# Storing a layer's reciprocals row by row instead of once per pair

## The chip, the core and the metric

The kernel runs on one core of a Trainium2 chip. The metric is the device time of a run in microseconds. Before the change the median of three runs is 3098.26 us (3097.44 to 3100.63).

## The reference

Two attention layers with residuals on x of shape (1, 128, 256, 256), read as 128 rows of 256 tokens with 256 channels, each over a group norm of the whole input. The change is in layer 1:

```python
def _L1_conv_ref(x, w_in, b_in, w_out, b_out, band):
    ...                                     # NUM_HEADS = 4, D = 64, F = 256 tokens
    qkv = x2 @ w_in.T + b_in
    q, k, v = jnp.split(qkv, 3, axis=-1)
    ...
    scores = jnp.einsum('bhid,bhjd->bhij', q, k) / jnp.sqrt(jnp.asarray(D, x.dtype))
    keep = jnp.abs(i - j) <= band           # band = 16
    scores = jnp.where(keep, scores, -jnp.inf)
    attn = jax.nn.softmax(scores, axis=-1)
    out = jnp.einsum('bhij,bhjd->bhid', attn, v)
    ...
    y = out @ w_out.T + b_out

x = x + _L0_conv_ref(_gn(x), ...)
x = x + _L1_conv_ref(_gn(x), ..., 16)
```

The sum of the exponentials of each token and head divides its output. The kernel takes the reciprocal of that sum, and keeps it for a check at the end.

## The kernel before

The kernel has a fast version, `fast_kernel`, and a general one that runs only where checks on the numbers fail; only the fast one runs here. Layer 0 writes its result x1 to memory. Layer 1, from about 1980 us on, works on *pairs* of rows (`NP` = 64 pairs). Everything in its loop is ordered by hand: every engine gets its instructions in the order of the program, and SyncE issues all of the loop's transfers from one queue, in that order too.

A pair p goes through four turns of the loop:

- As `n3` (turn p-3) it is made: `Pair1.__init__` issues its loads, four of 128 KB into `xs` (line 1930, in runs of 32 floats), which has 3 buffers, and one of 512 KB into `xt` (line 1935), which has 6. In the same turn, some three quarters through it, `turn` transposes `xs` on VectorE (line 1943).
- As `nn` it is normalised (`centre`, line 1948) and its differences and biased residual are made on GpSimd.
- As `nxt` its q, k and v come from seven products each (`product`, lines 1995 and 1999; `join`, line 2015).
- As `now` it has its scores (line 2052, rows 0 and 1), the exponentials and the mask by the band, and `apply(0)` for row 0: outputs (line 2077) and sums (line 2085). `invert(0)` takes the reciprocal of row 0's sums into `rv[:, 0, :]` (line 2108) and `weigh(0)` multiplies (line 2113). These two are the last of the turn in the program.
- As `was`, in the turn after, it has `apply(1)`, `invert(1)` and `weigh(1)` for row 1, and its output projection (line 2170). As `old` the residual is added on GpSimd (line 2186) and the result stored (line 2187).

The order of SyncE's work in a turn p of the loop is therefore: the loads of pair p+3, the output of pair p-2 (waits for GpSimd), and in `weigh(1)` the store of both rows' reciprocals of pair p-1 into `rsum1` (line 2118). The store takes every 32nd partition of `rv`, 4 partitions of 2 KB. A few turns before the end `load_sums` reads all of `rsum1` back for the check. The last `LATE` = 8 pairs check their reciprocals in place and store nothing.

On TensorE a turn has two stretches of many small instructions: both `scores` with `was.apply(1)` at its start, and `now.apply(0)` in its middle. The rest are larger products.

Of the kernel before, what the change touches and what calls it, by code (L numbers as in the profile page):

```python
# [16 lines left out]
P = 128  # L17
# [4 lines left out]
def bcast(ap, axis, n):  # L22

    ap = ap.unsqueeze(axis)
    shape = list(ap.shape)
    shape[axis] = n
    return ap.broadcast_to(shape)
# [746 lines left out]
def fast_kernel(  # L774
# [25 lines left out]
    nc = tc.nc  # L800
# [9 lines left out]
    NP = S // 2  # L810
# [1031 lines left out]
    DH = P // H1  # L1842
    QB = 32
    LATE = 8
    rsum1 = dram.tile([NP, H1, 2, I], F32, name="rsum1")
    with tc.tile_pool(name="l1", bufs=2) as sb, tc.tile_pool(
# [74 lines left out]
        class Pair1:  # L1921
# [188 lines left out]
            def weigh(self, r):  # L2110
                rv, odd = self.rv, self.odd
                oT = sb.tile([P, 2, I], F32, name="oT1", tag="oT", bufs=3)
                nc.vector.tensor_tensor(oT, odd, bcast(rv[:, r, :], 1, 2), ALU.mult)
                self.oT[r] = oT
                if self.p >= NP - LATE:
                    look(late, self.rv[:, r, :], 1e-16)
                if r == 1 and self.p < NP - LATE:
                    nc.sync.dma_start(rsum1[self.p].rearrange("q r i -> q (r i)"), rv[0:P:DH].rearrange("q r i -> q (r i)"))

            def out_row(self, r):  # L2120
                for b in range(NB):
# [91 lines left out]
        def look(queue, src, lo):  # L2213

            at = cols[0]
            cols[0] += 1

            def low():
                above = sm.tile([P, I], F32, name="above", tag="above", bufs=1)[:, : src.shape[1]]
                nc.vector.tensor_scalar(above, src, lo, None, ALU.is_gt)  # L2220
                nc.vector.tensor_reduce(ok[:, 0, at : at + 1], above, AX.X, ALU.min)

            queue += [lambda: nc.vector.tensor_reduce(ok[:, 1, at : at + 1], src, AX.X, ALU.max), low]
# [238 lines left out]
```

## Time and profile before

| | |
|---|---|
| median of three runs | 3098.26 us |
| time of the profiled execution | 3098.43 us |
| its span on the chip | 3096.7 us |
| TensorE matmul busy | 2991.3 us (97%) |
| TensorE weight load busy | 2088.0 us (67%) |
| VectorE busy | 2374.1 us (77%) |
| ScalarE busy | 1656.8 us (54%) |
| GpSimd busy | 2587.0 us (84%) |
| granted TensorE clock, mean | 0.987 |
| moved by DMA | 328.06 MB in 690787 packets |

In the profile PE is TensorE's matmuls, PEld its weight loads, DVE is VectorE, ACT ScalarE, POOL GpSimd and SP SyncE; a q behind an engine's name stands for its sequencer, which issues transfers. L2118 is line 2118 of the kernel. A row of waits has the instruction that waited, what ended the wait, the sum in us, how often and the longest. A row of the timeline has the start, the duration, the engine, the line and the tiles, written from read. "+9.2" in the text stands for 9.2 us after the first matmul of a pair's scores; pairs are counted by the turn in which they are `now`.

### The profile page before, as it was taken

The page shows a single profiled execution, that of the slowest core. Times are in us where ns is not written, and L with a number is a line of the kernel's source. Part 1 is how long each engine was busy: PE and PEld are TensorE (multiplying, and loading weights), DVE is VectorE, ACT ScalarE, POOL GpSimd, SP SyncE. Part 2 cuts the span into 40 slices and gives each one's busy share as a digit, 9 for nine tenths or more (in the row PEclk, how much of TensorE's full clock was granted, in tenths as well). Part 3 has the DMA queues.
Part 4 walks back from the last instruction along what each step waited for, and adds up shares of the span by engine and source line. Part 5 has one row for each costly group of instructions (what it writes and reads, how often), then busy time and mean ns, then how long its engine had stood idle before and what let it go on. Part 6 is the DMA issues. An engine that isn't in the chain of part 4 may idle for free.

```text
span 3096.7 us, 83063 instructions
## 1 busy us (share of the span) xinstructions
PE 2991.3 (97%) x34386; PEld 2088.0 (67%) x34386; DVE 2374.1 (77%) x4075; ACT 1656.8 (54%) x2887; POOL 2587.0 (84%) x1950
## 2 busy tenths in 40 slices
PE   6689999999999999999999999899999999999998
PEld 4355555665555655555655555588888888888886
DVE  7987677777777777777777777688887877777787
ACT  3454544444444444444444444366666666666664
POOL 3469899898898888898888898588888888888885
PEclk9799999999999999999999999999999999999999
DMA  9952333323333332333333233433434343434341
GB/s 357 390 190 53 100 70 100 95 65 93 100 97 73 96 90 67 100 97 91 78 89 95 73 97 87 112 89 93 99 90 104 86 105 85 105 92 97 94 100 44
DMA packets 690787, 328.06 MB, mean 106 GB/s; under 512 B 538624, under 2 KB 639872, under 8 KB 689248
## 3 DMA queue, kind: packets, MB, share of 16 engines
q1 hardware_dynamic: 686000, 320.02, 38.8%
q8 instruction: 273, 4.47, 0.6%
q10 hardware_dynamic: 4400, 2.63, 0.3%
q14 instruction: 114, 0.93, 0.1%
HBM read 253.83 MB, written 68.74 MB: 104 GB/s over the span
## 4 chain that ended last, share of the span: by engine, by line
PE 89%; DVE 4%; DMA 4%; POOL 1%; issue 1%; ACT 1%; SPq 0%; ACTq 0%; POOLq 0%; DVEq 0%
PE ps_p L1364 21%; PE ps_qk L1999 12%; PE ps_sc L1401 9%; PE ps_ov L1436 8%; PE ps_v L1382 7%; PE ps_y L1490 7%; PE ps_su_y L2170 6%; PE ps_qk L1995 6%; PE ps_o L2077 4%; PE ps_su L1444 3%; PE ps_sc L2052 3%; PE ps_su_y L2085 2%; DMA xa<-in_x_dram 2%; DMA zt<-in_z_dram 1%; DVE st L1199 1%
## 5 line engine op out<-in xcount | busy, mean ns | idle before, releaser
L1425 POOL TENSOR_TENSOR eboth<-e 128x512 f32<-128x512 f32 x512 | 744.2, 1475 | 174.2 <-PE ps_su L1444 95.2
L1421 DVE TENSOR_TENSOR e<-ps_sc,eb 128x1024 f32<-128x1024 f32 x384 | 458.2, 1221 | 288.7 <-ACT ps_sc L1413 288.6
L1413 ACT ACTIVATE ps_sc<-ps_sc 128x1024 f32<-128x1024 f32 x384 | 375.4, 1007 | 435.8 <-PE ps_sc L1401 310.0
L2063 POOL TENSOR_TENSOR e<-e,bw 128x384 f32<-128x384 f32 x256 | 276.6, 1111 | 77.4 <-ACT e L2061 77.4
L1401 PE MATMUL ps_sc<-qT,kT 32*128 32x256 f32 x4096 | 293.9, 400 | 0.0
L1401 PEld LDWEIGHTS ps_sc<-qT,kT 32*128 32x128 f32 x4096 | 185.5, 184 | 101.5 <-issue 91.5
L1490 PEld LDWEIGHTS ps_y<-wo,oT 128*128 128x128 f32 x1024 | 194.2, 190 | 81.8 <-issue 44.0
L1436 PE MATMUL ps_ov<-e,v 128*32 128x256 f32 x4096 | 247.6, 382 | 1.1 <-DVE v L1388 1.1
L1364 PE MATMUL ps_p<-xnT,wq 128*128 128x512 f32 x512 | 247.5, 605 | 0.1
L1364 PE MATMUL ps_p<-xgT,wg 128*128 128x512 f32 x512 | 247.3, 605 | 0.0
L1490 PE MATMUL ps_y<-wo,oT 128*128 128x256 f32 x1024 | 242.0, 379 | 1.7 <-POOL oT L1480 1.7
L1382 PE MATMUL ps_v<-wv,xnT 128*128 128x256 f32 x1024 | 241.8, 379 | 0.0
L1364 PE MATMUL ps_p<-xnT,wk 128*128 128x512 f32 x512 | 240.7, 592 | 0.0
L1382 PEld LDWEIGHTS ps_v<-wv,xnT 128*128 128x128 f32 x1024 | 194.5, 190 | 54.0 <-issue 30.9
L2008 ACT ACTIVATE u<-ps_qk,bin_c 128x256 f32<-128x256 f32 x378 | 174.7, 477 | 93.0 <-PE ps_qk L1999 93.0
L2108 DVE RECIPROCAL rv<-sums 128x256 f32<-128x256 f32 x128 | 223.0, 1742 | 0.0
L1436 PEld LDWEIGHTS ps_ov<-e,v 128*32 128x32 f32 x4096 | 120.0, 109 | 109.4 <-issue 41.5
L1116 POOL TENSOR_TENSOR zrs<-zrs,mhalf 128x32 f32<-128x32 f32 (+1 forms) x19 | 87.9, 4631 | 114.4 <-DVE zrs L1109 114.4
L1371 ACT ACTIVATE gT<-ps_p,bg_c 128x512 f32<-128x512 f32 x128 | 87.9, 687 | 175.1 <-PE ps_p L1364 175.1
L1364 PEld LDWEIGHTS ps_p<-xnT,wk 128*128 128x128 f32 x512 | 97.2, 190 | 122.8 <-issue 122.6
L1999 PE MATMUL ps_qk<-dT,wst 128*128 128x256 f32 x756 | 173.5, 379 | 0.0
L1364 PEld LDWEIGHTS ps_p<-xnT,wq 128*128 128x128 f32 x512 | 91.9, 189 | 114.0 <-issue 112.0
(254 smaller groups left out, 7061.1 us busy)
## 6 DMA issues: line engine op xcount, KB each, us to landing
xa<-in_x_dram SPq DMA_DIRECT2D x8, 4096.0 KB
xt<-in_x_dram SPq DMA_DIRECT2D x64, 512.0 KB
x<-xo SPq DMA_DIRECT2D x16, 2048.0 KB
xt<-x SPq DMA_DIRECT2D x64, 512.0 KB
rvb<-rsum SPq DMA_DIRECT2D x252, 128.0 KB
xs<-x SPq DMA_DIRECT2D x252, 128.0 KB
out_dram<-yo SPq DMA_DIRECT2D x63, 512.0 KB
xs<-in_x_dram SPq DMA_DIRECT2D x248, 128.0 KB
```

The source lines that it names most:

```text
L1364: nc.tensor.matmul(ps, w[:, k, m * P : (m + 1) * P], getattr(self, src)[:, k, :], start=(k == 0), stop=(k == KC - 1),)
L1382: nc.tensor.matmul(self.ps_v[:, b * C : (b + 1) * C], self.xnT[:, k, t * P : (t + 1) * P], wv[:, k, :], start=(k == 0), stop=(k == KC - 1),)
L1401: nc.tensor.matmul(self.pss[q // 2][:, q % 2, b, :], self.kT[rs, c, r * I + b * P : r * I + (b + 1) * P], self.qT[rs, c, r * I : (r + 1) * I],
L1413: nc.scalar.activation(self.pss[a], ps, AF.Exp)
L1421: nc.vector.tensor_tensor(es[a], pss[a], eb[:, h : h + 2], ALU.mult)
L1425: nc.gpsimd.tensor_tensor(t, es[a][:, :, 0, :], es[a][:, :, 1, :], ALU.add)
L1436: nc.tensor.matmul(ov[q * D0 : (q + 1) * D0, c, :], self.v[:, r, b, h * D0 : (h + 1) * D0], es[q // 2][:, q % 2, b, :], start=(b == 0), st ...
L1490: nc.tensor.matmul(self.ps_y[:, b * C : (b + 1) * C], self.oT[r][:, k, b * P : (b + 1) * P], wo[:, k, :], start=(k == 0), stop=(k == KC - 1),)
L1995: nc.tensor.matmul(to[:, at], rhs[:, at], lhs, start=start and b == 0, stop=True, skip_group_check=True)
L1999: nc.tensor.matmul(to, lhs, rhs, start=start, stop=True, skip_group_check=True)
L2063: nc.gpsimd.tensor_tensor(e[:, q], e[:, q], bcast(bw.rearrange("p b w -> p (b w)"), 1, KC), ALU.mult)
L2108: nc.vector.reciprocal(self.rv[:, r, :], self.sums)
```

## The change

The store of a pair's reciprocals is no longer made once, with row 1. `weigh` stores its own row each time: row 0 at the end of turn p, and row 1 in the middle of turn p+1.

```diff
                 if self.p >= NP - LATE:
                     look(late, self.rv[:, r, :], 1e-16)
-                if r == 1 and self.p < NP - LATE:
-                    nc.sync.dma_start(rsum1[self.p].rearrange("q r i -> q (r i)"), rv[0:P:DH].rearrange("q r i -> q (r i)"))
+                if self.p < NP - LATE:
+                    nc.sync.dma_start(rsum1[self.p][:, r, :], rv[0:P:DH, r, :])
```

SyncE's order in a turn p becomes: the loads of pair p+3, the output of pair p-2, row 1 of pair p-1, row 0 of pair p. The bytes that are stored are the same.

## The prediction

> **What bounds the kernel now.** First the page: the busy shares and the chain of work that ended last.
>
> ```profile
> PE 2991.3 (97%) x34386; PEld 2088.0 (67%) x34386; DVE 2374.1 (77%) x4075; ACT 1656.8 (54%) x2887; POOL 2587.0 (84%) x1950
> ...
> q8 instruction: 273, 4.47, 0.6%
> ...
> PE 89%; DVE 4%; DMA 4%; POOL 1%; issue 1%; ACT 1%; SPq 0%; ACTq 0%; POOLq 0%; DVEq 0%
> ```
>
> TensorE is nearly always busy, and the chain is TensorE. A change to loads can only pay where TensorE stands still, so I ask where that is inside layer 1. The timeline gives the start of each pair's scores (L2052): 2400.96, 2418.39, 2435.13, 2451.88 us. Most pairs take exactly 16.74 us, the others 16.8 to 18.4. From pair 2 (2026.33) to pair 56 (2945.64) there are 54 pairs in 919.31 us, against 54 x 16.74 = 903.96: **15.35 us are lost**, 0.5% of the run. The waits of TensorE's weight loads from 2010 to 3010 us, and the chain around one slow pair (number 50, start 2842.69), say to what:
>
> ```profile
> PEld ps_o L2077 <- issue: 24.0, 70, 1.0
> ...
> PEld ps_su_y L2085 <- issue: 9.0, 13, 1.4
> ```
> ```profile
> 2851.10 0.31 PE ps_su_y L2085 x8
> 2851.41 1.06 issue
> 2852.47 0.52 PE ps_su_y L2085 x6
> ```
>
> "issue" means that the engine waited for nothing that the profile shows. It falls in the middle of `apply` (L2077, L2085), never on a row that names a load. I take it for instruction fetch: the DMA share by slices of time around that stop (columns: PE, PEld, DVE, ACT, POOL busy, clock, DMA share, GB/s) has one lone packet ahead of it,
>
> ```profile
> 2846.19:2849.94 3.75, 3.75 (x19) 3.13 (x17) 3.07 (x5) 2.39 (x6) 3.75 (x4) 1.00 0.00 0
> 2849.94:2850.94 1.00, 1.00 (x71) 0.84 (x75) 0.99 (x3) 1.00 (x3) 0.91 (x1) 1.00 0.06 16
> 2850.94:2851.44 0.50, 0.47 (x23) 0.10 (x8) 0.50 (x2) 0.45 (x1) 0.00 (x0) 1.00 0.00 0
> 2851.44:2852.44 1.00, 0.00 (x0) 0.00 (x0) 0.30 (x1) 0.00 (x0) 0.55 (x1) 1.00 0.63 216
> ```
>
> and that packet is of queue 8, "instruction", 16 KB. Listing the packets of queue 8 against TensorE's records: a pair has 622 records, a fetch comes every 256 or so, and 7 pairs (4354) are 17 fetches plus 2 records, so the pattern repeats every seventh pair. Each time TensorE stops it goes on 2.2 to 2.7 us after the start of the latest fetch (pair 50: fetch at 2850.08, on at 2852.47), and always 384 to 388 records after the same point of the stream. So a fetch needs about 2.35 us before its instructions can run. It hurts only where 256 instructions run faster than that: in the **first burst** (both scores and `apply(1)`, 0 to 3 us into a pair) and the **second** (`apply(0)`, about 8.0 to 9.4 us into it).
>
> Where the loads are today: SyncE's part of the timeline,
>
> ```profile
> 2409.14 0.38 SPq L2187 DMA_DIRECT2D out_dram<-yo  x1
> 2409.62 0.54 SPq L2118 DMA_DIRECT2D rsum<-rv  x1
> 2410.21 2.93 SPq L1930 DMA_DIRECT2D xs<-x  x4
> 2413.18 1.98 SPq L1935 DMA_DIRECT2D xt<-x  x1
> ```
>
> Pair 24 began at 2400.96, so the loads are issued 9.25 us into it, 55% through. By the packets, the out store moves from +9.1 to +10.8, xs from +10.8 to +14.3 or, with a fetch in between, +15.9, and xt until +15.9 to +17.4. From there to +9 of the next pair the DMA engines do nothing but fetch: **both bursts now have the engines to themselves**.
>
> **What the Trainium skill says.** "Runtime: NRT & Kernel Launch", Instruction fetch mechanics: instructions come in blocks of 16 KiB (256), which the engine's sequencer fetches by its own DMA queue while it runs the block before. The trace agrees: 4.47 MB in 273 packets is 16.4 KB each, and 68,772 matmuls and weight loads over 256 make 269. "DMA: Bandwidth & Descriptors", Anatomy of one DMA: a wait for a semaphore is held by the issuing sequencer, not by the DMA engines. The trace agrees: nothing on SyncE passes the out store while it waits for POOL (483.9 us in all). Same page, Queues, rings and completion order: a DMA engine takes turns between queues packet by packet, a packet being 9 to 17 descriptors as a rule and at most 64. No row here shows the packets' size; that fetches do start amid 128-byte descriptors, the trace shows (19 of them, below).
>
> **The change part by part.** *Stores.* One store of 8 KB for a pair becomes two of 4 KB: 56 more issues of about 0.54 us (L2118), 30 us of SyncE. SyncE waits up to 8.6 us in a pair for the out store's data, so they cost nothing; without that cover SyncE would still have 16.74 us for 0.38 + 2 x 0.54 + 2.93 to 4.2 + 0.66 to 2.0, under 8. The row-0 store reads a row that the second reciprocal doesn't write; were that wait there all the same, it would have from +3.7 to +5.8, where the reciprocal of row 1 starts (2441.00 in pair 26, begun 2435.13).
>
> *The new wait.* The row-0 store stands at the end of a pair's program and waits for `invert(0)`, whose reciprocal ends 3.17 us into the next pair by the clock (pair 26: 2436.56 + 1.74), or 2.18 from pair 27 on, where the checks ahead of it have run out. Queued behind it on SyncE: four xs loads and the xt load of the coming pair, then the out store and the row-1 store. So the xs loads move from +9.25 of one pair to +3.8 (+2.8) of the next, **11 to 12 us later**, not sooner.
>
> *Who waits for them.* The transpose (L1943) reads xs 12.8 us into the pair. Now: four issues, then data 0.9 us after the first (out store: 2409.14, data +9.1), 3.5 to 5.1 us of it: landed at +8.2 to +9.8. At least 3 us are left: cost 0. xt is read a pair later: 0. The out store waits for POOL until +8.2 and now also for the xt issue, until +7.4 to +9; its buffer is written again a pair later: 0.
>
> *What the loads now lie beside.* xs moves from about +4.7 to +8.2 (+3.7 to +7.2), xt and the out store until about +12: across the second burst. Fetches that start there and have nothing to spare: pairs 8, 15, 22, 29, 36, 43, 50 (at +6.83 to +7.40; TensorE on at +9.2 to +9.8), and pair 1 by the same count: **8 fetches**. Those of the next family (pairs 3, 10 ... 52, at +7.2 to +8.5) are wanted 0.9 to 2.1 us after they are usable: 0.
>
> Price of one delay: the trace has no tight fetch under load, so bounds. 4096 descriptors over 16 engines in 3.5 us are 13.7 ns each: 17 of them 0.23 us, 64 of them 0.88 us. For the lower end: the packet of a fetch itself took 0.88 to 1.1 us mostly in the 128-byte stream as on idle engines. A gain is excluded: the engines are idle there today. I take half the ceiling, 0.4 us: 8 x 0.4 = **+3.2 us** (1.8 to 7.0).
>
> What is given back: in the first burst three fetches (pairs 21, 26, 33) start within 0.05 us of the end of xt. At 0.1 us each: **-0.3 us**. Sum +2.9 us on the profiled execution's 3098.43 (span 3096.7); that one is 0.17 above the median 3098.26, so on the median: 3101.
>
> **The rivals.**
> *Slower, clearly:* a fetch is held until the 128-byte stream has passed, instead of taking turns. Then the 8 fetches wait from about +7.0 to +8.2 or later, 1.2 to 2 us each: +10 to +16, **3110**. It decides from 0.78 us a fetch (6.2 / 8). For it: fetches of pairs 13 and 55 come 0.6 to 1.2 us later than their place in the stream suggests, with loads in flight. Against: 19 fetches start at +9.9 to +12.9 amid load.
> *No effect:* fetches pass at no cost. **3098.3**. For it: their unchanged length under load.
> *Faster:* the tail of xt is what holds the first burst's fetches, which start anywhere from +16.5 to +0.85. If all nine late ones started at +16.5, they would give back 5.2 us, and shorter packets (six take 1.2 to 1.3 rather than 0.95 us) 1.9 more: **3091 to 3093**. Against: most start 0.2 to 1.1 us after the last load has ended, and those at +16.5 start just after `join` frees the bank for `scores(1)`, so it is TensorE's sequencer that is late.
> *Loads too late* for the transpose: a microsecond per pair, about **3150**; 3 us of margin speak against it. That the change doesn't move the loads: SyncE is in order, so only if the reciprocal were not last; it is.
>
> **How the numbers follow.** A measurement of this kernel tells about 0.2% (6.2 us) from no change. Small cost 0.45 (0.07 of it beyond 0.2%), no effect 0.15, held fetches 0.21, faster 0.16 (0.13 beyond 0.2%), late loads 0.03. Faster 0.13, same 0.38 + 0.15 + 0.03 = 0.56, slower 0.07 + 0.21 + 0.03 = 0.31. The range, 3093 to 3110, takes in both ends of the delay's price, most of the faster case and half of the held fetches.
>
> **What would show it.** SyncE's timeline: store, four xs and xt at +2.8 to +3.8, no wait of the transpose on a DMA; the pair's floor still 16.74; in every seventh pair a stop in L2085 that is longer by 0.2 to 0.9 us; the first burst's stops as before. I am wrong if the floor of all pairs moves, if pairs without a tight fetch begin to stop in the second burst, or if the first burst's stops go.

## The result, and the profile after

**3106.14 us** (median of ten runs, 3102.42 to 3112.05) against 3098.49 for the kernel before (3096.68 to 3100.78): a ratio of **1.0025**, 95% interval 1.0017 to 1.0033. The change makes the kernel 7.6 us slower, and its runs spread more than twice as wide. The profiled execution took 3109.16 us (span 3107.4), in the upper half of the ten, so its differences are larger than the median's.

The first lines of the page, and the waits of TensorE's weight loads from 2010 to 3010 us for which the profile shows no releaser:

```profile
PE 2984.2 (96%) x34386; PEld 2085.0 (67%) x34386; DVE 2374.1 (76%) x4075; ACT 1657.2 (53%) x2887; POOL 2585.3 (83%) x1950
...
q8 instruction: 273, 4.47, 0.6%
```
```profile
PEld ps_o L2077 <- issue: 26.5, 71, 1.0
...
PEld ps_su_y L2085 <- issue: 13.4, 12, 2.8
...
PEld ps_qk L1999 <- issue: 10.9, 27, 1.9
```

The work and the 273 instruction blocks are the same, and the granted clock, taken over the whole run, is no lower (0.989 for 0.987). Longer are the stops in L2085, the end of `apply` (13.4 us for 9.0), and in L1999, the products behind it (10.9 for 7.5 over the same stretch before). SyncE's timeline shows where the loads went; columns are start and duration in us, issuer, line, transfer and how often:

```profile
2391.45 0.38 SPq L2187 DMA_DIRECT2D out_dram<-yo  x1
2391.94 11.80 SPq L2118 DMA_DIRECT2D rsum<-rv  x2
2403.79 2.76 SPq L1930 DMA_DIRECT2D xs<-x  x4
2406.60 0.72 SPq L1935 DMA_DIRECT2D xt<-x  x1
2408.20 0.38 SPq L2187 DMA_DIRECT2D out_dram<-yo  x1
```

Pair 24 starts at 2400.02. The two stores (row 1 of a pair, then row 0 of the next, which waits 11 us) stand in one row, and the loads come 3.77 us into the pair instead of 9.25. From pair 27 on it is 2.80.

The floor of a pair is still 16.74 us, and no transpose waits for a DMA: the profile lists no wait before L1943. (VectorE waits for an output store to leave its buffer four times, 2.0 us in all, and never before the change; the prediction put this at nothing, and the chain of work does not pass through it.) The time is lost in the pairs with a stop. Their sums over the floor, from the starts of the scores:

| pairs | before | after |
|---|---|---|
| 8, 15, 22, 29, 36, 43, 50 | 8.25 us | 18.96 us |
| the other 47 from 2 to 55 | 7.05 us | 8.28 us |

So +10.7 of the profiled execution's +10.7 us lie in seven pairs; the rest (+1.2 in the other pairs, +1.1 in pairs 56 to 60, -2.5 ahead of pair 2) cancels. Of the -2.5, 1.2 is pair 1, which takes 16.74 us for 17.95: it has a fetch at +3.1 where it had one at +7.8, and no stop. The long pieces in which the chain of work after the change stood at "issue" (start, us) are one in every seventh pair, 15 to 50; before, only one piece of this chain, of 1.06 us in pair 50, was long enough to be listed:

```profile
2252.94 1.29 issue
2373.40 1.29 issue
2493.77 2.13 issue
2615.05 1.04 issue
2735.11 2.16 issue
2858.60 2.43 issue
```

Pair 43 (start 2726.12) by slices of time, and the chain through it:

```profile
2732.12:2733.37 1.25, 1.25 (x8) 1.09 (x7) 1.25 (x2) 0.54 (x2) 1.25 (x1) 1.00 1.34 208
2733.37:2733.87 0.50, 0.50 (x11) 0.17 (x16) 0.50 (x1) 0.39 (x1) 0.50 (x1) 1.00 0.43 63
2733.87:2734.87 1.00, 1.00 (x75) 0.88 (x76) 0.99 (x4) 1.00 (x3) 0.41 (x1) 1.00 1.09 383
2734.87:2735.37 0.50, 0.23 (x9) 0.00 (x0) 0.50 (x1) 0.21 (x1) 0.00 (x0) 1.00 0.69 238
```
```profile
2734.80 0.31 PE ps_su_y L2085 x9
2735.11 2.16 issue
2737.26 0.75 PE ps_su_y L2085 x5
2738.01 3.34 PE ps_qk L1999 x8
```

The last three numbers of a slice are the granted clock, the DMA share and GB/s. xs runs out at 2733.4, and just as the second burst begins xt takes every engine (share 1.09, 383 GB/s). The instruction fetch of this pair starts at +8.65 (2734.77) by the packets of queue 8, when xt is nearly through; in the kernel before it started at +6.82 on idle engines. TensorE goes on 2.5 us after that start, as ever. The eight products behind the stop take 3.34 us where they took 1.92 in the same pair before:

```profile
2734.13 1.92 PE ps_qk L1999 x8
```

There is no gap between these products; TensorE runs slowly. The granted clock, third from the end in the slice that follows, is at half for 3.41 us from just after the stop, which costs some 1.7 us:

```profile
2737.42:2740.83 3.41, 3.41 (x12) 2.35 (x8) 0.42 (x1) 1.63 (x4) 1.73 (x3) 0.50 0.03 8
```

In this profile it happens in layer 1's loop only here, and not after the stops of pairs 29 and 50, which are as long; the last section says what sets them apart.

### The profile page after: what moved, and what is told of

It reads as the page before. It is cut to its first block, busy times and chain, and to the rows that moved or that the text cites. A ratio compares the mean times of both kernels' runs of the same rounds, so it can differ in the third digit from the quotient of the medians.

```text
span 3107.4 us, 83227 instructions
## 1 busy us (share of the span) xinstructions
PE 2984.2 (96%) x34386; PEld 2085.0 (67%) x34386; DVE 2374.1 (76%) x4075; ACT 1657.2 (53%) x2887; POOL 2585.3 (83%) x1950
## 4 chain that ended last, share of the span: by engine, by line
PE 89%; DVE 4%; DMA 4%; POOL 1%; issue 1%; ACT 1%; SPq 0%; ACTq 0%; POOLq 0%; DVEq 0%
PE ps_p L1364 21%; PE ps_qk L1999 12%; PE ps_sc L1401 9%; PE ps_ov L1436 7%; PE ps_y L1490 7%; PE ps_v L1382 7%; PE ps_su_y L2170 6%; PE ps_qk L1995 6%; PE ps_o L2077 4%; PE ps_su L1444 3%; PE ps_sc L2052 3%; PE ps_su_y L2085 2%; DMA xa<-in_x_dram 2%; DMA zt<-in_z_dram 1%; DVE st L1199 1%
## 5 line engine op out<-in xcount | busy, mean ns | idle before, releaser
L1999 PE MATMUL ps_qk<-dT,wst 128*128 128x256 f32 x756 | 173.4, 379 | 0.0
```

The source lines that it names most:

```text
L1999: nc.tensor.matmul(to, lhs, rhs, start=start, stop=True, skip_group_check=True)
```

## The experiments

The theory: the moved loads meet the instruction fetches of the second burst. Rivals: the extra stores; the reordering as such; 128-byte pieces rather than large ones; a wait on data that looks like a fetch.

**Row 0's store behind the loads.** Row by row as after the change, but holding nothing up (the main lines of the edit):

```diff
 # in weigh: row 1 alone is stored here; row 0, in the loop behind the loads of n3:
+                was.store_row(0)
                 now.scores(0)
```

> The store of row 0 is still made on its own, but stands behind the loads of the next turn in the program, so that it holds nothing up; two stores a pair as after the change, the loads at +9 as before it. If the cost is the moved loads (they meet TensorE's instruction fetches in the second burst): 3098 us, within 2 of the kernel before, and the stops of every seventh pair as before, TensorE on again at +9.2 to +9.8. If the cost is the 56 extra stores and their issues: 3104 to 3108, as after the change.

3099.07 us against 3099.22 for the kernel before; ratio 0.9999 (0.9990 to 1.0008). The 56 more stores cost nothing that can be measured; **the place of the loads is the whole cost**, as far as an interval of about 2.5 us to either side can tell. In this run the seven tight fetches start at +6.9 to +7.9, a little later than in the profile of before: that much a clean execution varies. Its seven pairs lose 11.3 us, and against this profile too (3101.11 us) the change's loss lies in them: 7.7 of 8.1 us.

**The checks behind the reciprocal.**

```diff
-                some_checks(2 if p > 0 else 0)
                 now.invert(0)
                 now.weigh(0)
+                some_checks(2 if p > 0 else 0)
```

> As after the change, but the two checks of a turn come behind the reciprocal and the weighing of row 0, so that in pairs up to 26 too the row-0 store is free about 1 us sooner and the loads start at +2.8 instead of +3.8. Then xs (128-byte pieces) is through by +7.3 and xt (1-KB pieces) and the output are in the engines when the second burst's fetches start. If a fetch waits longer behind 1-KB pieces than behind 128-byte ones (2 us against 0.5 to 0.9): pairs 8, 15 and 22 lose about 1.5 us more each, pairs 3, 10, 17 and 24 about 0.3, 5 to 8 us in all: 3111 to 3114. If the later pairs lose more for another reason than what is in the engines at +7 to +9: 3106, no change from after. If sooner loads are simply better: under 3104.

3111.16 us, ratio 1.0040 (1.0025 to 1.0054), from five runs: 5 us above the change, as the theory of the large pieces has it, but the two intervals overlap, so that it is slower than the change is not shown. The loads of pairs up to 26 do start at +2.8 (pair 22, begun at 2369.62):

```profile
2372.41 2.75 SPq L1930 DMA_DIRECT2D xs<-x  x4
2375.21 0.67 SPq L1935 DMA_DIRECT2D xt<-x  x1
```

Where the time went is not as expected. Pairs 2 to 26 lose 11.6 us, for 8.1 after the change, but pairs 8, 15 and 22 just 0.7 of the difference, not 1.5 each; most is in the families behind them (a family is every seventh pair; pairs 4, 10, 11, 13, 18, 24), whose fetches now also start late (3, 10, 17 and 24 at +9.3 to +9.8). Pairs 27 to 55 lose less, 15.2 us for 19.2: here the fetches of pairs 29, 36 and 50 got in ahead of xt, at +7.1 to +7.2, with packets of 1.5 to 1.7 us. This run alone does not tell the sizes of the pieces apart.

**The same reordering in the kernel before,** as a control:

> A control for the run with the checks behind the reciprocal: the same reordering in the kernel before the change, where no load waits for row 0's reciprocal. If the reordering acts through the loads alone: 3098 to 3100, no difference. If it costs something on VectorE by itself: 3103 or more, and the 5 us that the reordering cost after the change would not be the loads'.

3098.02 against 3097.93 us, ratio 1.0001 (0.9992 to 1.0010). By itself the reordering costs nothing that can be measured.

**xt later, xs as moved.** In the loop (the loads of the first three pairs stay ahead of it):

```diff
-                nc.sync.dma_start(self.xt, rows(x1[s0 // GB], s0 % GB, 2))   # in Pair1.__init__
+                n3.load_xt()                                                  # behind was.weigh(1)
```

> As after the change, but the xt load (1-KB pieces) is issued behind the row-1 store, at about +9.5, where it was in time before; xs stays at +2.8 and +3.8. If it is the 1-KB pieces of xt that hold the fetches from +7 to +9: in pairs 29, 36, 43, 50 the fetch starts at +6.8 to +7.5 again and the run takes 3099 to 3102; the early pairs 8, 15, 22 (xs still in the engines) keep their 0.5 to 0.9 us. If xs matters as much, or the output store does: 3104 to 3108.

3098.75 us, ratio 0.9999 (0.9990 to 1.0008): the whole cost is gone with xt out of the way, although the data of xs still move at +5.2 to +9.6 (pair 22) and +4.3 to +7.5 (pair 43). (The seven pairs lose 12.3 us in its profile, 1.0 more than with row 0 behind the loads; pair 1 has no stop, as after the change.) The late fetches start at +7.2 to +8.0 again, and those of the next family at +7.5 to +8.2. The 0.5 us that the early pairs' fetches still lose to xs (+7.4 to +7.8) is too little to be seen in the total.

**xt in four transfers, and in two.** The same bytes in the same 1-KB pieces, at the same place:

```diff
-                nc.sync.dma_start(self.xt, rows(x1[s0 // GB], s0 % GB, 2))
+                two = rows(x1[s0 // GB], s0 % GB, 2)
+                for t in range(2 * NB):                  # in two: range(0, 2 * NB, 2), t : t + 2
+                    nc.sync.dma_start(self.xt[:, t : t + 1, :], two[:, t : t + 1, :])
```

> As after the change, but the xt load is made in four transfers of 128 KB instead of one of 512 KB: the same bytes in the same 1-KB pieces, 8 for each DMA engine and transfer instead of 32. If a fetch has to let one transfer's pieces on its engine pass (32 x 50 ns = 1.6 us) and then takes its turn, it now waits for 8 (0.4 us): the late pairs' stops shrink by about 1 us each, 3100 to 3103. If a fetch has to wait until its engine has no data left at all, however cut: 3105 to 3108, and a little more for the longer issue (3 x 0.66 us of SyncE, hidden).

> As after the change, with the xt load in two transfers of 256 KB: 16 pieces of 1 KB for each DMA engine and transfer. One transfer cost 7.6 us, four cost nothing that can be measured. If a fetch waits for what one transfer has queued on its engine: 16 x 50 ns = 0.8 us instead of 1.6, the fetches of pairs 29 to 50 start at about +8, and the run takes 3100 to 3103, between the two. If only transfers above some size are harmful, and this one is below it: 3099, as with four; if above: 3106.

In four: 3099.15 us, ratio 1.0001 (0.9993 to 1.0010), better than I expected. In two: 3100.38, ratio 1.0010 (1.0001 to 1.0019). One transfer, two, four: +7.6, +2.4 and about 0 us, with intervals of 5.3 to 10.2, 0.3 to 5.9 and -2.2 to 3.1: one and four differ clearly, and that two lies between is not clear of the noise. The tight fetches of pairs 29, 43 and 50 started at +9.1, +8.6 and +9.4 with one transfer, at +8.3, +8.1 and +7.4 with two, at +8.1, +7.4 and +7.4 with four. (Pair 36 is left out: with one transfer its fetch got in ahead of xt at +7.2, with two it came at +10.3 and the pair had no stop; with four it started at +7.7.) So it is not 512 KB in the second burst that hurts, but 512 KB in *one* transfer. Pair 43 (start 2724.27) with four:

```profile
2731.51:2732.01 0.50, 0.50 (x11) 0.17 (x14) 0.50 (x1) 0.38 (x1) 0.50 (x1) 1.00 0.88 277
2732.01:2733.01 1.00, 1.00 (x76) 0.89 (x76) 0.99 (x4) 1.00 (x3) 0.40 (x1) 1.00 0.87 287
2733.01:2733.51 0.50, 0.25 (x10) 0.00 (x0) 0.50 (x1) 0.23 (x1) 0.00 (x0) 1.00 0.32 86
```
```profile
2733.26 1.06 issue
```

The stop is back to 1.06 us. Open stays why: a fetch may get its turn when one transfer's pieces on its engine are through, or it may use the gaps that the four issues leave (the share is 0.87 here, 1.09 with one transfer). That xs, also four transfers, runs at a share of 1.34 without gaps and still lets a fetch in after 0.5 us speaks for turns; for xt itself nothing here tells the two apart.

**Is it the fetch at all?** Nine small matmuls ahead of the loop, so that the borders of the blocks fall 36 records earlier in every pair:

```diff
+            for _ in range(9):
+                busy(64)
             nc.tensor.matmul(ps[0][:, :G], avg, st1[:, :, 1], start=True, stop=True)
```

> As after the change, with 9 small matmuls (64 columns, 36 records with their weight loads, results unused) put into TensorE's stream ahead of layer 1's loop; nothing in the loop is touched. If the stops are instruction fetches, the borders of the 256-instruction blocks fall 36 records earlier in every pair: the long stops of the second burst leave pairs 8, 15, 22, 29, 36, 43, 50 and come to pairs 3, 10, 17, 24, 31, 38, 45, 52, with the same sizes (0.5 to 1 us beyond clean in the early ones, 1 to 3 in the late ones), and the whole takes 3103 to 3110. If they come from a wait on data (a buffer, a semaphore, a load), the loop is the same and they stay at 8, 15 ... 50.

3105.11 us, ratio 1.0023 (1.0014 to 1.0031). The long pieces of the chain at "issue":

```profile
2403.22 1.29 issue
2523.36 2.13 issue
2645.84 1.04 issue
2765.96 1.06 issue
2885.93 1.88 issue
```

Their pairs are 24, 31, 38, 45 and 52 (begun at 2394.20, 2514.36, 2637.12, 2757.21 and 2877.17). Pairs 8, 15, 22 lose under 0.1 us now, 29, 36, 43 and 50 0.3 to 0.6; the eight pairs 3, 10 ... 52 lose 15.5 us, for 4.6 after the change. Not a line of the loop differs, so no wait on data in the loop can have moved the stops: **they are instruction fetches.** The records say the same: counted in TensorE's records, every stop of over 0.25 us in pairs 2 to 55 ends at the same place of a block of 256 (10 before, 18 after, 9 here). Pair 10 loses 1.1 us as expected; pairs 3 and 17 were also expected and show no stop. After the stops of pairs 31 and 52 the granted clock is at half for 3.41 us, as in pair 43 after the change.

**A version that is faster than both.** In the kernel before, five such matmuls (20 records):

> The kernel before the change, with 5 small matmuls (20 records) ahead of layer 1's loop, so that the borders of the instruction blocks fall 20 records earlier in every pair. A try for a version that beats both: by the fetches' places the second burst's tight family (96 to 108) goes to 76 to 88, where it still is tight, and of the first burst's three families (424, 462, 498 and up) one, at 404 to 418, leaves the tight region while the last stays on its border. Expected gain 1 to 4 us: 3094 to 3097. If the place of the borders does not matter before the change: 3098.

3094.07 against 3096.83 us, ratio 0.9991 (0.9985 to 0.9998), as expected in size. The stops in L2085 shrink from 9.0 to 2.4 us over the same stretch (a matmul's line is shifted by two):

```profile
PEld ps_o L2079 <- issue: 24.0, 71, 0.6
...
PEld ps_qk L2001 <- issue: 6.2, 20, 0.6
PEld ps_su_y L2087 <- issue: 2.4, 5, 0.8
```

I had expected the gain in the first burst; it came in the second: the seven pairs lose 1.7 us for 8.25. One of its 21 runs took 11,569.82 us, left out of the ratio; what happened in it was not found (the general version of the kernel may have run), so the version is shown for what it tells, not to be used as it is.

## Why the prediction was right, and where it was off

- **Place and cause: right.** The time was to be lost in every seventh pair, in L2085, by fetches that meet the loads in the second burst, with the pair's floor, the stores and the transpose unchanged. The table, the chain and the shift by 36 records show the first, the run with row 0 behind the loads that the stores cost nothing.
- **Direction right, size short.** 3101 was forecast, +2.9 us; measured +7.6, inside the range. It lies between "small cost" and "held fetches": by the dividing line of 0.78 us a fetch the early three (0.6) are the first and the late four (1.6) the second, to which it gave a chance of 0.21. That the time fell inside the range owes something to the range's width and to luck, since more than half of the cost came by that less likely path.
- **The term that failed: the price of one delay,** "I take half the ceiling, 0.4 us", bounded at 0.88. I worked it out from the 128-byte pieces of xs alone (13.7 ns each), although the same text puts xs at +3.7 to +7.2 from pair 27 on, so that the fetches at +6.8 to +7.4 meet xt. Its 32 pieces of 1 KB on an engine take 1.6 us (512 KB in that time, by the packets of before: 50 ns each). The count was not the fault, for 32 pieces lie within the 64 of the bound; the price of a piece was. Measured: in pairs 8, 15 and 22, amid xs, the fetches start 0.6 us later than before (mean +7.67 against +7.07), near the 0.4; in pairs 29, 36, 43 and 50 1.6 us later (+8.58 against +7.00). That mean hides two cases: in pair 36 the fetch got in ahead of xt (+7.24), in the other three it waited for nearly all of xt and started 1.8 to 2.1 us later. Whether this is why the runs spread so wide is not shown. With 0.6 for three fetches and 1.6 for four the sum is 8.2 of the seven pairs' 10.7 us.
- **A term that was missing: the clock.** 1.7 us of the 10.7 are the half clock behind the stop of pair 43.
- **Pair 1, the eighth fetch:** wrong. It had a stop before, and none after the change, nor in any other run with the loads moved; it gave back 1.2 us.
- **"Those of the next family ... 0":** nearly. From pair 31 on these start at +9.2 to +9.7 and have lost their slack of 0.9 to 2.1 us; pairs 31, 38, 45 and 52 lose 3.0 us, for 1.7 before. In pairs 45 and 52 TensorE now stops behind the burst (L1999, 0.4 and 0.8 us), in pair 45 for the first time: the sign "pairs without a tight fetch begin to stop" came true, in small.
- **The given back 0.3 us:** not to be seen. First-burst fetches still start from +16.5 on although the loads have ended 4 us earlier, so the tail of the loads was not what held them, which is also what spoke against the faster rival.
- **The stores at nothing:** right (ratio 0.9999 in the first experiment).

## What to carry to other kernels

TensorE's stops that wait for "issue" inside bursts of small matmuls are worth listing against the packets of the instruction queue: if TensorE always goes on about the same time after a fetch began, and the stops move when records are put ahead of the loop, the stop is a fetch, and whatever transfer lies around its start is part of TensorE's path. Before moving a load, look at what else uses the DMA engines at the new place, and price a meeting by the largest single transfer there, not by the first one in the queue. Where a load has to lie beside such a burst, issue it in several smaller transfers: here that took away all of the cost that can be measured. And look at the granted clock behind a long stop: in three cases here a stop of about 2 us cost some 1.7 us more than its length.

## What the runs showed of the hardware

- The fetches of 16 KB in pairs 29, 36, 43 and 50 start 1.6 us later on average (up to 2.1) with a 512-KB transfer beside them, and 0.7 later with the same pieces in four transfers of 128 KB; with the loads at +9 they start 0.5 later in another profile (+7.6, about 0 and 0 us in all). I had not expected the cut of a transfer to matter to another queue.
- From the start of a fetch's packet to the first instruction of its block pass 2.2 to 2.7 us before the change and 2.2 to 2.9 after it (pair 43: 2.4 and 2.5); it is the start that a load delays, mostly, less the packet (0.9 us, up to 1.8 where it meets another stream).
- The place of the block borders alone, moved by 20 records, is worth 2.8 us (0.6 to 4.6) of 3097 in the kernel before.
- In each of the ten traces all changes of the granted clock lie on a grid of 3.41 us. In layer 1's loop it went to half for one step of the grid three times, each after a step in which TensorE's matmuls had stood still for 1.9 to 2.2 us (2.16 in pair 43 after the change, 2.13 and 1.88 in pairs 31 and 52 of the run shifted by 36 records). The steps with less, up to 1.85 us (pair 29 with xt in two), were not followed by it. The stops of pairs 29 and 50 after the change, 2.13 and 2.43 us long, each fall across two steps, with 1.3 and 1.7 us in the fuller one.
